# A graph layer's last stage: x1 of half of the rows added on TensorE and kept in PSUM, a quarter of the rows normalised by VectorE

## The chip, the cores and the metric

The kernel runs on one core of a Trainium2 chip. The metric is the device time of one execution in microseconds (us); lower is better. Engines are TensorE (PE; its weight loads are PEld), VectorE (DVE), ScalarE (ACT), GpSimd (POOL) and SyncE (SP), which issues the transfers here. The memory that TensorE writes to is PSUM: 8 banks of 512 fp32 numbers per partition, 128 partitions.

## The reference

`x` is (16, 1024, 256) in fp32: 16 batches, 1024 nodes, 256 channels. Two layers follow each other, each with a residual and a layer norm over the channels:

```python
x = _layernorm(x + _L0_gnn_ref(x, para, adj, kv_w))     # attention over a weighted graph
x = _layernorm(x + _L1_gnn_ref(x, adj, W1, b1, g1, be1, W2, b2, g2, be2))

def _L1_gnn_ref(features, A, W1, b1, g1, be1, W2, b2, g2, be2):
    ...
    agg = jnp.einsum('nm,bmd->bnd', A_hat, features)
    h = jax.nn.relu(_batchnorm(agg.reshape(-1, d) @ W1.T + b1, g1, be1))
    out = h @ W2.T + b2
    out = _batchnorm(out, g2, be2)         # mean and variance over all 16 x 1024 rows
    return out.reshape(b, n, -1)
```

The first layer's output is called x1 below. The change concerns the last line of the first block for layer 1: batch norm of `out`, the sum with x1, and the layer norm. The batch norm needs statistics over all rows, so no row can be finished before the last `out` is known.

## The kernel before

The function `fast_path` does everything (a second function, for denominators out of range, isn't run with these inputs). Layer 0 goes over 16 batches with attention in bursts on TensorE, ScalarE and VectorE, and stores x1 of each batch in DRAM. Then `aht` holds the normalised adjacency, and layer 1 computes the aggregate and the first linear map batch by batch, stores `h` in DRAM and collects statistics in `bn1_st`.

Two stages remain, and they are the ones that the change touches. In both the order of instructions on TensorE, ScalarE and VectorE is the order of the program (`manual_schedule`)[...]. The framework puts in the semaphore waits that the data need.

*Second linear map* (from L1431). For each batch `b`, `h` is loaded (`load_h`, two ahead), ScalarE applies batch norm 1 and relu to it in place (`scale_shift1`, L1387), and TensorE computes `out` transposed, in two halves `c` of 128 channels: eight matmuls of 512 columns (L1456) into a PSUM tile `po` of 1024 columns, which is two banks. VectorE adds the bias `b2` while it copies to `o2T[b]` (L1460) and collects `bn_stats` of both 512-column halves in `bn2_st` (L1464). All 16 `o2T` tiles stay in SBUF, 8 KB per partition each. After the last batch `coefficients2(c)` turns the statistics into a scale `sg2` and a shift `sh2` per channel: `bn_aggr` on VectorE (L1227), five small operations on GpSimd (L587 to L1231).

*Last stage* (from L1473). x1 of a batch comes back from DRAM as `xf[b]`, with 8 groups `n` of 128 rows along the free dimension. Seven buffers hold it: three in pool `xp` (batches 0 to 2, loaded during the stage before) and four in `fin2`. For each batch:

- `scale_shift(b)`: ScalarE applies scale and shift to `o2T[b]` in place, two instructions of 1024 columns (L1485), one for each half of the channels.
- `residual2(b)`: for each of four pairs of row groups, TensorE transposes four 128x128 blocks back to rows (L1497, tile `pf`, one bank; four such tiles take turns), VectorE adds x1 and writes the sum over `xf` (L1502, 512 columns), and takes `bn_stats` of each of the two row groups (L1504). Then GpSimd computes the reciprocal standard deviation and the negative mean times it, for all 8 groups at once, in ten small operations (L1510 to L1519).
- `finish(b)`: ScalarE normalises each of the 8 row groups (L1526, 256 columns), writing over `o2T[b]`, and SyncE stores the batch (L1530) and then loads x1 of batch `b + 7` (L1428) into the buffer that has come free.

The loop at L1536 puts them in the order `residual2(b)`, `scale_shift(b + 1)`, `finish(b - 1)`, so that GpSimd has the time of one batch to make its coefficients.

Of the kernel before, what the change touches and what calls it, by code (L numbers as in the profile page):

```python
# [10 lines left out]
F32 = mybir.dt.float32  # L11
I32 = mybir.dt.int32
AF = mybir.ActivationFunctionType
ALU = mybir.AluOpType
AX = mybir.AxisListType
PSUM = bass.MemoryType.PSUM
DRAM = bass.MemoryType.DRAM

P = 128
HALF = 512  # L20
# [495 lines left out]
def fast_path(  # L516
# [19 lines left out]
    nc = tc.nc  # L536
    B, N, C = x.shape
    H = 4
    D = C // H
    NCH = N // P  # L540
    CC = C // P
    FH = W1.shape[0]
    HC = FH // P
    scale = float((1.0 + 1e-06) / (np.sqrt(D) + 1e-06))

    const = ctx.enter_context(tc.tile_pool(name="const", bufs=1))
# [4 lines left out]
    def open_psum():  # L551

        stack = ExitStack()
        for tag in "sto":
            psum[tag] = stack.enter_context(tc.tile_pool(name=f"ps_{tag}", bufs=2, space=PSUM))
        return stack
# [3 lines left out]
    def tile_s(name):  # L560
        return psum["s"].tile([P, N], F32, tag="s", name=name)

    def tile_t(name):
        return psum["t"].tile([P, HALF], F32, tag="t", name=name)

    def tile_o(name):
        return psum["o"].tile([P, HALF], F32, tag="o", name=name)
# [7 lines left out]
    ident = const.tile([P, P], F32, name="ident")  # L575
# [95 lines left out]
    H0, H1 = slice(0, HALF), slice(HALF, N)  # L671
# [3 lines left out]
    cols = {}  # L675
# [24 lines left out]
    with (  # L700
# [10 lines left out]
        st = {}  # L711
# [404 lines left out]
        with tc.manual_schedule(engines={mybir.EngineType.PE, mybir.EngineType.Activation, mybir.EngineType.DVE}):  # L1116
# [48 lines left out]
            for j in range(len(bursts)):  # L1165
                b, u = j // PERB, j % PERB
# [30 lines left out]
            j = len(bursts)  # L1197
# [14 lines left out]


    w1T, w2T = wl["w1T"], wl["w2T"]
    bn1_st = const.tile([P, HC, 2 * B, 6], F32, name="bn1_st")
    bn2_st = const.tile([P, CC, 2 * B, 6], F32, name="bn2_st")

    def batchnorm(stats, gamma, beta, k, name):

# [15 lines left out]
    with (  # L1235
# [9 lines left out]
        def bank(name):  # L1245
            return ps8.tile([P, HALF], F32, tag="bank", name=name)

        def temps(k):
            return lambda key, name: strt.tile([P, HALF], F32, tag=f"{key}{k}", name=f"{key}_{name}")


        wS = strt.tile([P, 4, C], F32, name="wS")
# [133 lines left out]
        def scale_shift1(h, k):  # L1386
            nc.scalar.activation(  # L1387
                h, h, AF.Relu, bias=sh1[:, k : k + 1], scale=sg1[:, k : k + 1]
            )
# [3 lines left out]
        for k in range(HC):  # L1393
            ps = [bank(f"ph_{k}_{half}") for half in range(2)]
            for c in range(CC):
                for half, hs in enumerate((H0, H1)):
                    nc.tensor.matmul(
                        ps[half], w1T[:, c, k * P : (k + 1) * P], t[:, c, hs],
                        start=(c == 0), stop=(c == CC - 1),
# [11 lines left out]
        nc.gpsimd.dma_start(h_d[B - 1], ht)  # L1411

    graph.close()
    ctx.enter_context(open_psum())

# [2 lines left out]
    with tc.tile_pool(name="o2p", bufs=1) as o2p:  # L1420
        o2T = [
            o2p.tile([P, CC, N], F32, tag=f"o2_{b}", name=f"o2_{b}") for b in range(B)
        ]
        xf = {}

        def load_x1(b, pool, tag):
            xf[b] = pool.tile([P, NCH, C], F32, tag=tag, name=f"xf_{b}")
            nc.sync.dma_start(xf[b], x1_d[b])  # L1428

        coefficients2, sg2, sh2 = batchnorm(bn2_st, cols["g2"], cols["be2"], CC, "bn2")  # L1430
        with (  # L1431
            tc.tile_pool(name="hl", bufs=2) as hl,
            tc.manual_schedule(
                engines={mybir.EngineType.PE, mybir.EngineType.Activation, mybir.EngineType.DVE}
            ),
        ):
            hs_of = {0: h0}

            def load_h(b):
                ht = hl.tile([P, HC, N], F32, tag="hl", name=f"hl_{b}")  # L1440
                nc.sync.dma_start(ht, h_d[b])
                hs_of[b] = [ht[:, k, :] for k in range(HC)]

            load_h(1)
            for b in range(B):
                if b + 2 < B:
                    load_h(b + 2)
                if b + 1 < B:
                    for k in range(HC):
                        scale_shift1(hs_of[b + 1][k], k)  # L1450
                h = hs_of.pop(b)
                for c in range(CC):
                    ps = tile_s(f"po2_{b}_{c}")
                    for k in range(HC):
                        for hs in (H0, H1):
                            nc.tensor.matmul(  # L1456
                                ps[:, hs], w2T[:, k, c * P : (c + 1) * P], h[k][:, hs],
                                start=(k == 0), stop=(k == HC - 1),
                            )
                    nc.vector.tensor_scalar(  # L1460
                        o2T[b][:, c, :], ps, cols["b2"][:, c : c + 1], None, ALU.add
                    )
                    for half, hs in enumerate((H0, H1)):
                        nc.vector.bn_stats(bn2_st[:, c, 2 * b + half, :], o2T[b][:, c, hs])  # L1464
                    if b == B - 1:
                        coefficients2(c)
                if b >= B - 3:
                    load_x1(b - (B - 3), xp, "x")

        with (  # L1473
            tc.tile_pool(name="fin2", bufs=4) as fin2,
            tc.manual_schedule(
                engines={mybir.EngineType.PE, mybir.EngineType.Activation, mybir.EngineType.DVE}
            ),
        ):
            for b in range(3, 7):
                load_x1(b, fin2, "xf")  # L1480

            def scale_shift(b):
                for c in range(CC):
                    o = o2T[b][:, c, :]
                    nc.scalar.activation(  # L1485
                        o, o, AF.Identity, bias=sh2[:, c : c + 1], scale=sg2[:, c : c + 1]
                    )

            def residual2(b):
                xt = xf[b]  # L1490
                st = small.tile([P, NCH, 6], F32, tag="ln_st", name=f"st_l1_{b}")
                for pair in range(NCH // 2):
                    pt = tile_t(f"pf_{b}_{pair}") if pair % 2 else tile_o(f"pf_{b}_{pair}")
                    for j in range(2):
                        n = 2 * pair + j
                        for c in range(CC):
                            nc.tensor.transpose(  # L1497
                                pt[:, j * C + c * P : j * C + (c + 1) * P],
                                o2T[b][:, c, n * P : (n + 1) * P], ident,
                            )  # L1500
                    xs = xt[:, 2 * pair : 2 * pair + 2, :].rearrange("p n c -> p (n c)")
                    nc.vector.tensor_add(xs, pt, xs)  # L1502
                    for n in (2 * pair, 2 * pair + 1):
                        nc.vector.bn_stats(st[:, n, :], xt[:, n, :])  # L1504

                me, qe, mo, qo = (st[:, :, k] for k in (1, 2, 4, 5))
                w = small.tile([P, 4, NCH], F32, tag="ln_w", name=f"w_l1_{b}")
                rstd, nmr, dif, var = (w[:, k, :] for k in range(4))
                pool = nc.gpsimd
                pool.tensor_tensor(nmr, me, mo, ALU.add)  # L1510
                pool.tensor_tensor(dif, me, mo, ALU.subtract)
                pool.tensor_tensor(var, qe, qo, ALU.add)
                pool.tensor_scalar(var, var, 1.0 / C, EPS, ALU.mult, ALU.add)
                pool.tensor_tensor(dif, dif, dif, ALU.mult)
                pool.tensor_scalar(dif, dif, 0.25, None, ALU.mult)
                pool.tensor_tensor(var, var, dif, ALU.add)
                pool.tensor_tensor(rstd, var, mhalf, ALU.pow)
                pool.tensor_tensor(nmr, nmr, rstd, ALU.mult)
                pool.tensor_scalar(nmr, nmr, -0.5, None, ALU.mult)  # L1519
                return rstd, nmr  # L1520

            def finish(b, rstd, nmr):
                xt = xf.pop(b)
                y = o2T[b].rearrange("p c n -> p (c n)").rearrange("p (n c) -> p n c", c=C)
                for n in range(NCH):
                    nc.scalar.activation(  # L1526
                        y[:, n, :], xt[:, n, :], AF.Identity,
                        bias=nmr[:, n : n + 1], scale=rstd[:, n : n + 1],
                    )
                nc.sync.dma_start(out[b].rearrange("(n p) c -> p n c", p=P), y)  # L1530
                if b + 7 < B:
                    load_x1(b + 7, *((fin2, "xf") if 3 <= b < 7 else (xp, "x")))

            scale_shift(0)
            coeffs = {}
            for b in range(B):  # L1536
                coeffs[b] = residual2(b)
                if b + 1 < B:
                    scale_shift(b + 1)
                if b:  # L1540
                    finish(b - 1, *coeffs.pop(b - 1))
            finish(B - 1, *coeffs.pop(B - 1))


# [41 lines left out]
```

## Time and profile before

The time is 2651.31 us, the median of three runs (2650.74 to 2654.38); the profiled execution has a span of 2651.3 us and a mean granted TensorE clock of 0.981.

| engine | busy us | share of the span | instructions |
|---|---|---|---|
| PE | 2553.7 | 96% | 12966 |
| PEld | 1110.1 | 42% | 12966 |
| DVE | 1600.2 | 60% | 2160 |
| ACT | 1126.8 | 43% | 1349 |
| POOL | 336.2 | 13% | 407 |

TensorE is busy nearly throughout, but not at the end: in the page's 40 slices of the span the last two digits of its row are 6 and 4, where the rest are 8 or 9, and the granted clock falls there too. By line, the chain of work that ended last has 8% of the span in L1456, 2% in L1526, and 1% each in L1485 and L1504. A row of the groups reads: line, engine, operation, out<-in by the program's names, shapes, count, then the busy time in us and the mean ns of one, then the idle time just before, with what ended most of it. Shares of the whole span say little on a stage of 120 us; for it the same views are cut to a window.

### The profile page before, as it was taken

Reading aid. Unit: us, or ns where it says so; the run is one execution under the profiler, and the core shown is the slowest. Engines: PE = TensorE matmul, PEld = TensorE weight load, DVE = VectorE, ACT = ScalarE, POOL = GpSimd, SP = SyncE. Lnnn points to the kernel's source line nnn. Section 1 sums busy time; section 2 is a strip of 40 time slices with the busy share of each in tenths; the row PEclk is TensorE's granted clock in tenths of the full one; section 3 lists DMA queues with packets and bytes.
Section 4 is the critical chain, followed back from the end, with each engine's and each line's share of the span. In section 5 each row is a group of like instructions: output and inputs, shape, how many; then the busy total and the mean of one; then the engine's idle time right before and its main releaser. Section 6 shows DMA issues by size and latency. Waiting matters only on the chain. (4 is left out here: it accounts for less than half of the span.)

```text
span 2651.3 us, 31994 instructions
## 1 busy us (share of the span) xinstructions
PE 2553.7 (96%) x12966; PEld 1110.1 (42%) x12966; DVE 1600.2 (60%) x2160; ACT 1126.8 (43%) x1349; POOL 336.2 (13%) x407
## 2 busy tenths in 40 slices
PE   8999999999999999999999999999999999999964
PEld 4443444444434434444444343344444444444443
DVE  5465665756656657666566576765655655533376
ACT  5363563654645636545446354410101001233368
POOL 0001000100100011001000100321222211100044
PEclk9999999999999999999999999999999999999975
DMA  4001101001011011010110110112122122353367
GB/s 143 2 9 41 33 10 41 21 22 33 9 41 33 9 41 33 10 41 3 39 33 9 41 49 1 41 64 95 80 95 95 66 92 82 137 202 143 149 222 240
DMA packets 134557, 168.94 MB, mean 64 GB/s; under 512 B 86785, under 2 KB 120065, under 8 KB 124033
## 3 DMA queue, kind: packets, MB, share of 16 engines
q1 hardware_dynamic: 129568, 116.47, 14.2%
q0 software_dynamic: 4832, 50.34, 4.6%
q8 instruction: 103, 1.69, 0.3%
q14 instruction: 54, 0.43, 0.0%
HBM read 99.36 MB, written 67.44 MB: 63 GB/s over the span
## 5 line engine op out<-in xcount | busy, mean ns | idle before, releaser
L908 ACT ACTIVATE p<-ps 128x1024 f32<-128x1024 f32 x512 | 495.7, 1020 | 179.5 <-PE ps L903 142.9
L933 DVE TENSOR_TENSOR acc<-acc,p 128x1024 f32<-128x1024 f32 x384 | 483.2, 1258 | 61.0 <-ACT p L908 32.4
L903 PE MATMUL ps<-qT,kT 64*64 64x512 f32 x4096 | 490.6, 594 | 1.4 <-ACT p L908 1.4
L924 PE MATMUL po<-p,v 64*64 64x512 f32 x4096 | 485.3, 589 | 0.0
L805 PE MATMUL pg<-wg,x 128*128 128x512 f32 x960 | 425.2, 596 | 0.0
L979 POOL TENSOR_TENSOR x<-x,o 128x512 f32<-128x512 f32 x64 | 109.5, 1711 | 1434.8 <-DVE o L974 1434.8
L924 PEld LDWEIGHTS po<-p,v 64*64 64x64 f32 x4096 | 156.7, 133 | 282.8 <-issue 282.6
L805 PEld LDWEIGHTS pg<-wg,x 128*128 128x128 f32 x960 | 177.6, 190 | 226.9 <-issue 203.3
L903 PEld LDWEIGHTS ps<-qT,kT 64*64 64x64 f32 x4096 | 146.1, 132 | 280.2 <-issue 231.5
L817 ACT ACTIVATE qT<-qT 128x512 f32<-128x512 f32 x64 | 40.3, 631 | 482.0 <-DVE qT L814 481.9
L1456 PE MATMUL po<-hl,w12T 128*128 128x512 f32 x512 | 220.3, 592 | 3.1 <-ACT hl L1387 2.3
L814 DVE SCALAR_TENSOR_TENSOR qT<-pg,para_s 128x512 f32<-128x512 f32 x64 | 43.9, 689 | 271.1 <-PE pg L805 269.8
L793 DVE SCALAR_TENSOR_TENSOR wg<-wg,adj_s 128x1024 f32<-128x1024 f32 x128 | 153.1, 1217 | 15.5 <-ACT wg L789 15.5
L784 ACT ACTIVATE wg<-crow,ccol 128x1024 f32<-128x1024 f32 x128 | 146.6, 1146 | 11.8 <-DMA crow<-c 11.8
L1456 PEld LDWEIGHTS po<-hl,w12T 128*128 128x128 f32 x512 | 97.1, 190 | 126.3 <-issue 120.5
L789 ACT ACTIVATE wg<-wg 128x1024 f32<-128x1024 f32 x128 | 135.5, 1060 | 2.6
L1387 ACT ACTIVATE hl<-hl,bn_sh,bn_sg 128x1024 f32<-128x1024 f32 x64 | 74.3, 1229 | 135.0 <-DMA hl<-h 133.6
L855 PE MATMUL pv<-kvw_s,xT 128*128 128x256 f32 x512 | 124.0, 385 | 1.6 <-ACT kT L846 1.6
L1460 DVE TENSOR_SCALAR o<-po,col_b 128x1024 f32<-128x1024 f32 x32 | 41.1, 1284 | 139.1 <-PE po L1456 139.1
L842 PE MATMUL pk<-xT,kvw_s 128*128 128x512 f32 x256 | 120.3, 592 | 0.0
L855 PEld LDWEIGHTS pv<-kvw_s,xT 128*128 128x128 f32 x512 | 94.9, 190 | 51.9 <-issue 27.6
L1286 PE MATMUL a_agg<-ahT,x1l 128*128 128x512 f32 x240 | 108.1, 593 | 1.1 <-ACT agg L1104 1.1
(151 smaller groups left out, 2625.4 us busy)
## 6 DMA issues: line engine op xcount, KB each, us to landing
h<-hw POOLq DMA_DIRECT2D x16, 2048.0 KB, 6.6
hl<-h SPq DMA_DIRECT2D x15, 2048.0 KB
x<-x POOLq DMA_DIRECT2D x16, 1024.0 KB, 4.2
x1l<-x SPq DMA_DIRECT2D x16, 1024.0 KB
xf<-x SPq DMA_DIRECT2D x16, 1024.0 KB
out_dram<-o SPq DMA_DIRECT2D x16, 1024.0 KB
x<-in_x_dram SPq DMA_DIRECT2D x15, 1024.0 KB
crow<-c SPq DMA_DIRECT2D x15, 512.0 KB
```

What stands on the lines that cost most here:

```text
L784: nc.scalar.activation(w, s["crow"], AF.Abs, bias=s["ccol"][:, n : n + 1])
L789: nc.scalar.activation(w, w, AF.Tanh, scale=0.5)
L793: nc.vector.scalar_tensor_tensor(w, w, 1.0, adj_s[:, n, :], op0=ALU.subtract, op1=ALU.mult)
L805: nc.tensor.matmul(ps, xt[:, n, c * P : (c + 1) * P], s["wg", n][:, hs], start=(n == 0), stop=(n == NCH - 1),)
L842: nc.tensor.matmul(ps, kvw_s[:, c, kc * P : (kc + 1) * P], s["xT"][:, c, hs], start=(c == 0), stop=(c == CC - 1),)
L855: nc.tensor.matmul(pt[:, j * C : (j + 1) * C], s["xT"][:, c, n * P : (n + 1) * P], kvw_s[:, c, C : 2 * C], start=(c == 0), stop=(c == CC - 1),
L903: nc.tensor.matmul(ps[kh * D : (kh + 1) * D, hd * HALF : (hd + 1) * HALF], kT[r, pr, ks], qT[r, pr, qh * HALF : (qh + 1) * HALF], start=Tr ...
L908: nc.scalar.activation(p, ps, AF.Exp)
L924: nc.tensor.matmul(g["po"][kh][hd * D : (hd + 1) * D, :], s["v"][r, m, h * D : (h + 1) * D], p[r, hd * HALF : (hd + 1) * HALF], start=(m = ...
L933: nc.vector.tensor_add(g["acc"], g["acc"], p)
L979: nc.gpsimd.tensor_tensor(xs, xs, o.rearrange("p n h d -> p n (h d)"), ALU.add)
L1456: nc.tensor.matmul(ps[:, hs], w2T[:, k, c * P : (c + 1) * P], h[k][:, hs], start=(k == 0), stop=(k == HC - 1),)
```

## The change

It reorders the end of the kernel in five ways.

- The last bias add (batch 15, second half of the channels) goes from VectorE to ScalarE, in two halves of 512 columns, each in a bank of its own.
- The first `scale_shift(0)` is done in four pieces of 512 columns, first both channel halves of the first four row groups, so that these can be transposed while the rest is scaled.
- For row groups 4 to 7 the sum with x1 is made by TensorE in PSUM: a matmul of `xf` (512 columns, two row groups) with the identity starts the bank (`add_x1`), and the transposing matmuls of `o2T` add to it (`start=False`). They are ordinary matmuls with the identity as moving operand, no longer transposes[...]. The sum stays there, in a tile `held` of two banks, three of which take turns, until `finish`. VectorE's add of these row groups goes; `bn_stats` reads PSUM. For row groups 0 to 3 all is as it was, with two PSUM tiles `ps_sum` in place of four.
- In `finish` VectorE normalises row groups 0 and 1, ScalarE groups 4 to 7 out of PSUM and then 2 and 3.
- The pools of PSUM of the stage before are closed, since `held` and `ps_sum` need all 8 banks; `bn1_st` and `bn2_st` move from the pool of constants to pools that live only as long as they are needed.

The aim is to take work from ScalarE and VectorE, the two busy engines of this stage, and give it to TensorE, which waits there, and to shorten the way from the last matmul to the first residual.

```diff
-    bn1_st = const.tile([P, HC, 2 * B, 6], F32, name="bn1_st")
-    bn2_st = const.tile([P, CC, 2 * B, 6], F32, name="bn2_st")
...
+        bn1_st = strt.tile([P, HC, 2 * B, 6], F32, name="bn1_st")
...
-    ctx.enter_context(open_psum())
+    part_psum = open_psum()
...
+        bn2_st = o2p.tile([P, CC, 2 * B, 6], F32, name="bn2_st")
...
-                    nc.vector.tensor_scalar(
-                        o2T[b][:, c, :], ps, cols["b2"][:, c : c + 1], None, ALU.add
-                    )
+                    if b == B - 1 and c == CC - 1:
+                        for hs in (H0, H1):
+                            nc.scalar.activation(
+                                o2T[b][:, c, hs], ps[:, hs], AF.Identity,
+                                bias=cols["b2"][:, c : c + 1],
+                            )
+                    else:
+                        nc.vector.tensor_scalar(
+                            o2T[b][:, c, :], ps, cols["b2"][:, c : c + 1], None, ALU.add
+                        )
...
+        part_psum.close()
         with (
             tc.tile_pool(name="fin2", bufs=4) as fin2,
+            tc.tile_pool(name="ps_held", bufs=3, space=PSUM) as ps_held,
+            tc.tile_pool(name="ps_sum", bufs=2, space=PSUM) as ps_sum,
...
             def scale_shift(b):
-                for c in range(CC):
-                    o = o2T[b][:, c, :]
+                for hs in (H0, H1) if b == 0 else (slice(0, N),):
+                    for c in range(CC):
+                        o = o2T[b][:, c, hs]
...
+            held = {}
+
+            def add_x1(b, pair):
+                if b not in held:
+                    held[b] = ps_held.tile([P, N], F32, tag="held", name=f"held_{b}")
+                nc.tensor.matmul(
+                    held[b][:, (pair - 2) * HALF : (pair - 1) * HALF], ident,
+                    xf[b][:, 2 * pair : 2 * pair + 2, :].rearrange("p n c -> p (n c)"),
+                    start=True, stop=False, skip_group_check=True,
+                )
+
             def residual2(b):
...
-                for pair in range(NCH // 2):
-                    pt = tile_t(f"pf_{b}_{pair}") if pair % 2 else tile_o(f"pf_{b}_{pair}")
+                for pair in range(2):
+                    pt = ps_sum.tile([P, HALF], F32, tag="sum", name=f"pf_{b}_{pair}")
...
+                for pair in range(2, 4):
+                    if b:
+                        add_x1(b, pair)
+                    pt = held[b][:, (pair - 2) * HALF : (pair - 1) * HALF]
+                    for j in range(2):
+                        n = 2 * pair + j
+                        for c in range(CC):
+                            nc.tensor.matmul(
+                                pt[:, j * C + c * P : j * C + (c + 1) * P],
+                                o2T[b][:, c, n * P : (n + 1) * P], ident,
+                                start=False, stop=True, skip_group_check=True,
+                            )
+                        nc.vector.bn_stats(st[:, n, :], pt[:, j * C : (j + 1) * C])
...
             def finish(b, rstd, nmr):
-                xt = xf.pop(b)
+                xt, hx = xf.pop(b), held.pop(b)
...
-                for n in range(NCH):
+                for n in (0, 1):
+                    nc.vector.tensor_scalar(
+                        y[:, n, :], xt[:, n, :], rstd[:, n : n + 1], nmr[:, n : n + 1],
+                        ALU.mult, ALU.add,
+                    )
+                for n in (4, 5, 6, 7, 2, 3):
                     nc.scalar.activation(
-                        y[:, n, :], xt[:, n, :], AF.Identity,
-                        bias=nmr[:, n : n + 1], scale=rstd[:, n : n + 1],
+                        y[:, n, :], hx[:, (n - 4) * C : (n - 3) * C] if n >= 4 else xt[:, n, :],
+                        AF.Identity, bias=nmr[:, n : n + 1], scale=rstd[:, n : n + 1],
                     )
...
+            add_x1(0, 2)
+            add_x1(0, 3)
             scale_shift(0)
```

More of the change, by code (lines that the diff above doesn't have):

```diff
@@ L1482, in scale_shift @@
             def scale_shift(b):
-                for c in range(CC):
-                    o = o2T[b][:, c, :]
-                    nc.scalar.activation(
-                        o, o, AF.Identity, bias=sh2[:, c : c + 1], scale=sg2[:, c : c + 1]
-                    )
+                for hs in (H0, H1) if b == 0 else (slice(0, N),):
+                    for c in range(CC):
+                        o = o2T[b][:, c, hs]
+                        nc.scalar.activation(
+                            o, o, AF.Identity, bias=sh2[:, c : c + 1], scale=sg2[:, c : c + 1]
+                        )
[8 more added lines that the diff above has]
+                )
             def residual2(b):
@@ L1522, in finish @@
             def finish(b, rstd, nmr):
-                xt = xf.pop(b)
+                xt, hx = xf.pop(b), held.pop(b)
                 y = o2T[b].rearrange("p c n -> p (c n)").rearrange("p (n c) -> p n c", c=C)
-                for n in range(NCH):
+                for n in (0, 1):
+                    nc.vector.tensor_scalar(
+                        y[:, n, :], xt[:, n, :], rstd[:, n : n + 1], nmr[:, n : n + 1],
+                        ALU.mult, ALU.add,
+                    )
+                for n in (4, 5, 6, 7, 2, 3):
                     nc.scalar.activation(
-                        y[:, n, :], xt[:, n, :], AF.Identity,
-                        bias=nmr[:, n : n + 1], scale=rstd[:, n : n + 1],
+                        y[:, n, :], hx[:, (n - 4) * C : (n - 3) * C] if n >= 4 else xt[:, n, :],
+                        AF.Identity, bias=nmr[:, n : n + 1], scale=rstd[:, n : n + 1],
                     )
```

## The prediction

> **What bounds the kernel now.** I read, in this order, the groups of instructions of the last 270 us, the windows of the last stage, the timeline of one batch, and the chain of waits. The change lies behind the last `po` matmul (it ends near 2531.7 us), so only some 120 of the 2651.3 us can move much. First the groups: line, engine, out<-in, count, then busy us and mean ns of one, then idle us and its releaser.
>
> ```profile
> L1526 ACT ACTIVATE o<-xf,w_l 128x256 f32<-128x256 f32 x128 | 64.5, 585 | 8.7 <-POOL w_l L1519 8.7
> L1497 PE MATMUL pf<-ident,o 128*128 128x128 f32 x256 | 57.0, 395 | 43.9 <-ACT o L1485 40.4 <-DVE xf L1502 3.5
> L1504 DVE BATCH_NORM_STATS2 st_l<-xf 128x6 f32<-128x256 f32 x128 | 48.2, 418 | 3.0
> L1502 DVE TENSOR_TENSOR xf<-pf,xf 128x512 f32<-128x512 f32 x64 | 43.3, 677 | 10.4 <-PE pf L1497 6.0 <-issue 4.4
> L1485 ACT ACTIVATE o<-o,bn_sh,bn_sg 128x1024 f32<-128x1024 f32 x32 | 37.6, 1226 | 18.9 <-POOL bn_sh L1231 18.9
> ```
>
> TensorE waits on ScalarE 40.4 us here, ScalarE almost only at the start (18.9 + 8.7). The windows give busy us of PE, PEld, DVE, ACT, POOL, then granted clock, DMA share, GB/s:
>
> ```profile
> 2580.00:2610.00 30.00, 18.12 (x79) 15.31 (x79) 26.36 (x59) 30.00 (x51) 17.18 (x50) 0.61 1.01 338
> 2610.00:2640.00 30.00, 14.28 (x64) 11.84 (x64) 23.56 (x52) 27.73 (x48) 16.99 (x50) 0.61 0.55 186
> ```
>
> ScalarE fills all 30.00 us, VectorE 26.36. The TensorE clock is 0.61 and the DMA share 1.01. One batch in the timeline (start us, us, instruction):
>
> ```profile
> 2604.87 4.03 ACT L1526 ACTIVATE o<-xf,w_l 128x256 f32<-128x256 f32 x8
> 2605.02 3.46 PE L1497 MATMUL pf<-ident,o 128*128 128x128 f32 x15 [0.66 <-ACT o L1485]
> 2606.01 0.69 DVE L1502 TENSOR_TENSOR xf<-pf,xf 128x512 f32<-128x512 f32 x1 [0.51 <-issue]
> 2606.81 0.75 DVE L1504 BATCH_NORM_STATS2 st_l<-xf 128x6 f32<-128x256 f32 x2
> 2607.48 0.67 DVE L1502 TENSOR_TENSOR xf<-pf,xf 128x512 f32<-128x512 f32 x1
> 2608.81 2.36 ACT L1485 ACTIVATE o<-o,bn_sh,bn_sg 128x1024 f32<-128x1024 f32 x2
> 2611.07 4.03 ACT L1526 ACTIVATE o<-xf,w_l 128x256 f32<-128x256 f32 x8
> ```
>
> The period is 2611.07 - 2604.87 = 6.20 us, all ScalarE: eight small activations cost (4.03 - 0.585) / 7 = 0.493 each in a row, 3.94 together, and two large ones 2.26. VectorE's pair period (an add, two statistics) is 1.38 (2607.48 to the next add at 2608.85); four are 5.52. The chain of waits gives the ends (start us, us, what):
>
> ```profile
> 2531.69 1.29 DVE o L1460
> 2533.01 1.30 DVE bn_st L1464 x2
> 2537.15 1.25 ACT o L1485
> 2539.38 0.70 DVE xf L1502
> ...
> 2637.93 1.68 POOL w_l L1517
> 2641.73 2.55 ACT o L1526 x5
> ```
>
> From the last `po` matmul to the first residual add it is 7.7 us. At the end the last statistics finish at 2636.14, GpSimd's ten small operations take 4.1 us, eight activations 4.04 (to 2644.28), the last store 7.0.
>
> [...] here the 128x512 copy from PSUM (L1017) takes 685 ns and the add of two SBUF operands (L666) 682, so I add nothing.
>
> **The change, part by part.**
>
> *Start.* ScalarE does the last bias add in halves (687 ns each by L1404, the same form), the first one matmul (0.43 us) before the last ends, and statistics of the first half overlap the second: statistics end near 2533.3 instead of 2534.3, 1.05 us earlier. The first scale and shift needs 0.63 (L817, 128x512) instead of 1.25 before TensorE may start. First residual add at 2539.4 - 1.05 - 0.6, about 2537.6. The two x1 matmuls of batch 0 lie in TensorE's wait for the coefficients: free.
>
> *ScalarE per batch:* 6 x 0.493 + 2.26 = 5.22, instead of 6.20. *VectorE's own work:* two pairs 2.76, four statistics at 0.335 (0.75 for two, less the tail) 1.34, two normalisations at 0.323 (L600, same form, eight in 2.67 us) 0.65: 4.75. By busy time all gets shorter.
>
> *The new wait.* For rows 4 to 7 the loop now writes row n with two transposing matmuls, and reads row n for its statistics, before it writes row n+1. Rows 4 and 5 share a bank, and 6 and 7. [...] the matmuls of row 5 must wait for the statistics of row 4, those of row 7 for row 6. Behind them in TensorE's queue stand the x1 matmul of the other bank, rows 6 and 7, and the whole next batch; VectorE waits for each in turn. Costs of the links:
> - statistics to matmul: 0.42 for the instruction + 0.05 (2546.96 to 2547.01 for add to transpose);
> - two matmuls to the statistics. Three transposes took 0.59 to VectorE's start at full clock (2561.62 to 2562.21) and 1.00 at half (2605.01 to 2606.01); one fewer is 0.11 or 0.21 less: 0.48 and 0.79. These are no longer in transpose mode; their weight load is 190 ns (L855) instead of 140 (L970) at full clock, so I add 0.07: 0.55 full, 0.86 half;
> - an x1 matmul of 512 columns: 0.43 full (220.3 us / 512), 0.85 half.
>
> From the start t of row 4's statistics, full clock / half clock: row 5's at t + 0.47 + 0.55 = 1.02 / 1.33. TensorE meanwhile streams row 5, the x1 matmul and row 6: 0.47 + 0.33 + 0.43 + 0.3 + 0.22 = 1.75 / 0.47 + 0.57 + 0.85 + 0.48 + 0.27 = 2.64, when row 6's statistics start. Row 7's follow 1.02 / 1.33 later: 2.77 / 3.97. Then 0.335 and the two normalisations 0.65: 3.76 / 4.96. With the 2.76 of the two pairs the period is 6.52 / 7.72. The next batch's first transposes fit behind row 7's statistics (ready near 3.4 / 4.8). Before had 6.20, so VectorE and TensorE in alternation become the bound and ScalarE's 0.98 us is worth nothing. I take the mean of the clocks, 7.1: this stage had full clock in about a fifth of its time at 0.61[...].
>
> *Sum.* Batch 0 needs no x1 matmul in the chain and no normalisation: about 5.8. Batch 1 starts at 2543.4, batch 15 at 2543.4 + 14 x 7.1 = 2642.8; its last statistics end 2.76 + 3.4 + 0.42 later, 2649.4. Then GpSimd 4.1, six activations 5 x 0.493 + 0.585 = 3.05, the store 7.0: 2663.6, rounded 2664. At full clock all through 2655, at half 2673. The last finish is 1.0 shorter than before; the normalisation by VectorE runs beside it.
>
> *Nothing gained or lost:* PSUM pools reopened (banks long read; the wait for coefficients hides it), three held tiles (one is freed two batches before it is asked for), the statistics tiles moved between pools (addresses only). DMA: nine load and store pairs at the 338 GB/s of before are 6.2 us each; a period of 7.1 asks for less.
>
> **Rivals.**
> - *No wait inside a bank* (only true overlaps of columns are ordered): then ScalarE sets 5.22, batch 15 starts at 2537.6 + 4.7 + 14 x 5.22 = 2615.4, its statistics end 4.3 later, plus 14.15: 2634. DMA, which is full at 338 GB/s, would end no earlier: 9 x 6.2 + 7 stores of about 3.4 from 2551.5 is 2631, and the last store's latency: so 2636. For it: the work by engine[...].
> - *Wait, but full clock:* 2655, about no change. [...] against it: 0.61 now with similar idle shares.
> - *Wait at half clock throughout:* 2673. [...]
>
> **How the numbers follow.** Wait with mixed clock (2658 to 2670) 0.66, with full clock (2650 to 2658) 0.09, with half clock (2670 to 2676) 0.10, no wait (2634 to 2641) 0.15. The range 2652 to 2676 holds 0.66 + 0.10 + most of 0.09, over 0.8. Above 2656.6 (0.2% over 2651.3) lie 0.66 + 0.10 + 0.03 = 0.79; within 0.2% 0.06; faster 0.15.
>
> **What would show it.** Right: in the changed profile the matmuls of rows 5 and 7 wait on the statistics, VectorE idles on them by some 2 to 3 us a batch, ScalarE has gaps, and the activations recur every 6.5 to 7.7 us. Start step: first add near 2537.6. Wrong: ScalarE without gaps and a period near 5.2; or a clock near 1.0; or VectorE waiting for the first transposes of a batch rather than for rows 5 to 7.

## The result, and the profile after

The changed kernel takes 2700.7 us, the median of four runs (2699.72 to 2703.64), against 2652.85 (2650.74 to 2655.2) for the kernel before beside it: a ratio of 1.0182, 95% interval 1.0164 to 1.02. It is slower, as the prediction said, but by 48 us where 12.7 were predicted; the time lies outside the range of 2652 to 2676. The profiled execution has a span of 2698.7 us.

The groups of the changed kernel's last 320 us (line, engine, operation, out<-in, shapes, count, then busy us and mean ns of one, then idle us just before and its releasers):

```profile
L1537 PE MATMUL held<-ident,o 128*128 128x128 f32 x256 | 52.4, 338 | 34.7 <-DVE st_l L1542 34.5 <-ACT o L1499 0.2
L1508 PE MATMUL held<-xf,ident 128*128 128x512 f32 x64 | 45.9, 810 | 9.2 <-DVE st_l L1542 7.9 <-ACT o L1463 1.4
L1569 ACT ACTIVATE o<-held,w_l 128x256 f32<-128x256 f32 x64 | 30.9, 563 | 74.8 <-POOL w_l L1557 69.4 <-DVE st_l L1542 5.4
L1542 DVE BATCH_NORM_STATS2 st_l<-held 128x6 f32<-128x256 f32 x64 | 27.4, 428 | 68.6 <-PE held L1537 68.6
L1522 PE MATMUL pf<-ident,o 128*128 128x128 f32 x128 | 21.2, 320 | 2.3 <-ACT o L1499 2.3
```

Three things are to be seen. VectorE now waits 68.6 us for the matmuls of `held` (L1542 on L1537), 4.3 a batch where 2 to 3 were forecast, and TensorE 34.5 + 7.9 us for the statistics (L1537 and L1508 on L1542): each waits for the other. ScalarE, which waited 8.7 us in its normalisation before, waits 74.8. And the counts: the code calls L1537 128 times (8 in each of 16 batches), the trace has 256; it calls L1508 32 times, the trace has 64. The transposes, L1522, are 128 in both.

A window of the last stage (busy us of PE, PEld, DVE, ACT, POOL, then granted clock, DMA share, GB/s):

```profile
2580.00:2610.00 30.00, 20.61 (x91) 14.34 (x90) 15.94 (x40) 17.07 (x26) 11.30 (x32) 0.81 0.63 211
```

ScalarE went from 30.00 of 30 us to 17.07, VectorE from 26.36 to 15.94, and no engine is full any more. The last part of one batch, in the timeline (start us, us, instruction, idle before and its releaser), shows the alternation:

```profile
2556.03 0.42 DVE L1542 BATCH_NORM_STATS2 st_l<-held 128x6 f32<-128x256 f32 x1
2556.50 0.71 PE L1537 MATMUL held<-ident,o 128*128 128x128 f32 x4 [2.08 <-DVE st_l L1542]
2557.25 0.43 DVE L1542 BATCH_NORM_STATS2 st_l<-held 128x6 f32<-128x256 f32 x1 [0.80 <-PE held L1537]
2557.74 2.08 PE L1508 MATMUL held<-xf,ident 128*128 128x512 f32 x2 [0.52 <-DVE st_l L1542]
2559.60 1.06 PE L1537 MATMUL held<-ident,o 128*128 128x128 f32 x4
2560.70 0.43 DVE L1542 BATCH_NORM_STATS2 st_l<-held 128x6 f32<-128x256 f32 x1 [3.02 <-PE held L1537]
2561.19 0.71 PE L1537 MATMUL held<-ident,o 128*128 128x128 f32 x4 [0.53 <-DVE st_l L1542]
2561.94 0.43 DVE L1542 BATCH_NORM_STATS2 st_l<-held 128x6 f32<-128x256 f32 x1 [0.81 <-PE held L1537]
2562.92 0.69 DVE L1527 TENSOR_TENSOR xf<-pf,xf 128x512 f32<-128x512 f32 x1
```

The four statistics are those of rows 4 to 7. Row 5's matmuls start 0.05 us after row 4's statistics end, row 7's after row 6's: the wait that was predicted. But the x1 matmul of the *other* bank (L1508, for rows 6 and 7) also starts only at 2557.74, 0.06 after row 5's statistics end. It was predicted to run beside them.

The chain of waits of the changed kernel at the start of the stage (start us, us, what):

```profile
2529.31 0.70 ACT o L1463
2530.03 1.30 DVE bn_st L1472 x2
2534.17 0.82 ACT o L1499
2535.62 0.70 DVE xf L1527
```

The last `po` matmul ends at 2529.27, so the way from it to the first residual add is 6.35 us, against 7.71 before (2531.67 to 2539.38). The tail, from the end of the last statistics (2684.33) to 2698.7, is 14.37.

**Where the time went.** The adds of the first pair of each batch recur every 9.35 us on average from batch 1 to batch 15 ((2675.34 - 2544.47) / 14); before it was 6.11 ((2630.45 - 2544.91) / 14, with 6.20 once steady).

### The profile page after: what moved, and what is told of

Read it like the earlier page. It is cut to its first block, busy times and chain, and to the rows that moved or that the text cites. A ratio compares the mean times of both kernels' runs of the same rounds, so it can differ in the third digit from the quotient of the medians.

```text
span 2698.7 us, 32309 instructions
## 1 busy us (share of the span) xinstructions
PE 2601.3 (96%) x13158; PEld 1138.4 (42%) x13158; DVE 1591.6 (59%) x2159; ACT 1111.1 (41%) x1321; POOL 339.0 (13%) x407
## 3 DMA queue, kind: packets, MB, share of 16 engines
q8 instruction: 105, 1.72, 0.3%
## 5 line engine op out<-in xcount | busy, mean ns | idle before, releaser
L817 ACT ACTIVATE qT<-qT 128x512 f32<-128x512 f32 x64 | 40.0, 630 | 482.0 <-DVE qT L814 482.0
L1457 PE MATMUL po<-hl,w12T 128*128 128x512 f32 x512 | 220.3, 593 | 3.3 <-ACT hl L1387 2.6
L855 PEld LDWEIGHTS pv<-kvw_s,xT 128*128 128x128 f32 x512 | 95.1, 190 | 52.9 <-issue 27.6
```

The costliest lines, as they stand in the source:

```text
L855: nc.tensor.matmul(pt[:, j * C : (j + 1) * C], s["xT"][:, c, n * P : (n + 1) * P], kvw_s[:, c, C : 2 * C], start=(c == 0), stop=(c == CC - 1),
L1457: nc.tensor.matmul(ps[:, hs], w2T[:, k, c * P : (c + 1) * P], h[k][:, hs], start=(k == 0), stop=(k == HC - 1),)
```

## The experiments

Two theories stood at the outset. A: the alternation of TensorE and VectorE in `held` costs the time, since reads and writes of the whole two-bank tile are kept in order, and since the links are longer than I took them (an ordinary fp32 matmul is two instructions in the trace). B: it is the amount of work that TensorE was given, in whatever order. The table has all runs (e3 and e8 leave out a part of the work): the median, the ratio to the kernel before on the same chip with its 95% interval, and the mean time from batch to batch (batch 1 to 15, first add to first add).

| run | us | ratio | us per batch |
|---|---|---|---|
| the change | 2700.7 | 1.0182 (1.0164 to 1.02) | 9.35 |
| e1_two_tiles | 2681.83 | 1.0107 (1.009 to 1.0124) | 7.98 |
| e2_stats_last | 2636.36 | 0.9936 (0.9919 to 0.9953) | 5.17 |
| e3_wait_single_pass | 2667.05 | 1.0049 (1.0032 to 1.0066) | 7.02 |
| e4_start_only | 2654.1 | 1.0001 (0.9992 to 1.0009) | 6.14 |
| e5_pair_stats_one_tile | 2666.77 | 1.0044 (1.0027 to 1.0061) | 7.15 |
| e6_pair_stats_two_tiles | 2632.29 | 0.9918 (0.9902 to 0.9935) | 5.06 |
| e7_vector_rows_only | 2653.06 | 0.9994 (0.9986 to 1.0003) | 6.16 |
| e8_wait_two_pass | 2692.95 | 1.014 (1.0123 to 1.0157) | 8.61 |
| e9_two_tiles_all_on_scalar | 2649.0 | 0.998 (0.9973 to 0.9987) | 5.95 |

### e1: `held` as two tiles of one bank

```diff
-            tc.tile_pool(name="ps_held", bufs=3, space=PSUM) as ps_held,
+            tc.tile_pool(name="ps_held", bufs=6, space=PSUM) as ps_held,
...
-                    held[b] = ps_held.tile([P, N], F32, tag="held", name=f"held_{b}")
+                t = ps_held.tile([P, HALF], F32, tag="held", name=f"held_{b}_{pair}")
+                held.setdefault(b, []).append(t)
...
```

> The changed kernel with the held PSUM tile split into two tiles of one bank each (six take turns), all orders as they are. In the trace of the changed kernel the x1 matmul of the second bank starts 0.05 us after the statistics of row 5 end, though these read the other bank. Theory A (the framework orders writes after reads over a whole tile): that matmul no longer waits, some 0.48 us a batch go (0.43 for the statistics and 0.05), 7 us in all: 2692 to 2695 us, and the x1 matmul starts before the statistics of row 5. Theory B (only the bank counts, and the wait has another cause): no change, 2699 to 2702 us.

It takes 2681.83 us. One batch in its timeline:

```profile
2579.74 0.71 PE L1537 MATMUL held<-ident,o 128*128 128x128 f32 x4 [0.53 <-DVE st_l L1542]
2580.29 1.02 PE L1508 MATMUL held<-xf,ident 128*128 128x512 f32 x2
2580.49 0.43 DVE L1542 BATCH_NORM_STATS2 st_l<-held 128x6 f32<-128x256 f32 x1 [0.81 <-PE held L1537]
2581.80 0.43 DVE L1542 BATCH_NORM_STATS2 st_l<-held 128x6 f32<-128x256 f32 x1 [0.87 <-PE held L1537]
```

The x1 matmul of the second bank (2580.29) now starts before row 5's statistics (2580.49), right behind row 5's matmuls, so its wait was one for the tile and not for the bank. From row 5's statistics to row 6's it is 1.31 us here and 2.09 in a batch of the change at full clock (2576.68 to 2578.77, granted clock 1.00): the wait for the tile is worth 0.78 a batch there. The mean fell by 1.37, more than expected. The rest of it goes with the clock: batches at full clock fell from 8.30 to 7.51 (2552.53 to 2567.55 has two, whose outer links take 1.22 to 1.24, as in the change at a granted clock of 0.99), by 0.79, while the mean stands 0.47 above the full-clock batch here and 1.05 in the change; from 2560 to 2590 the granted clock is 0.89 here and 0.81 there.

### e2: the statistics of rows 4 to 7 after all their matmuls

```diff
-                        nc.vector.bn_stats(st[:, n, :], pt[:, j * C : (j + 1) * C])
+                for n in range(4, 8):
+                    nc.vector.bn_stats(st[:, n, :], held[b][:, (n - 4) * C : (n - 3) * C])
```

> The changed kernel with the statistics of rows 4 to 7 issued after all matmuls of these rows. Same instructions, same arithmetic. Theory A (the alternation of writes and reads in a tile is the loss): TensorE runs a batch without stopping, 8 transposes, 4 x1 instructions and 16 transposing ones, at full clock about 0.9 + 1.7 + 2.0 = 4.7 us, so ScalarE's 5.2 or so sets the period: 2635 to 2650 us, faster than the kernel before. Theory B (the doubled fp32 instructions on TensorE are the loss whatever the order): at half clock they need 9.1 us, the period stays near 9, 2680 us or more.

It takes 2636.36 us, faster than before by 0.64%, with exactly the instructions of the change. Its window:

```profile
2560.00:2590.00 30.00, 27.11 (x168) 20.11 (x166) 27.71 (x70) 29.84 (x48) 21.20 (x58) 1.00 1.05 401
```

ScalarE is full again (29.84), TensorE is busy for 27.11 of 30 us at a clock of 1.00. Theory B falls: the same TensorE work, in another order, goes through in 5.17 us a batch. (Its clock is higher too, but at full clock a batch of the change still takes 8.30.)

### e3 and e8: the wait alone, with one or two instructions to a link

Both leave out x1 for rows 4 to 7, so TensorE has no x1 matmul; the rest of the change is kept. e3 fills `held` with transposes, e8 with ordinary matmuls. The diff of e3 (in e8 the call stays `nc.tensor.matmul`, with `start=True`):

```diff
-                    if b:
-                        add_x1(b, pair)
...
-                            nc.tensor.matmul(
+                            nc.tensor.transpose(
                                 pt[:, j * C + c * P : j * C + (c + 1) * P],
                                 o2T[b][:, c, n * P : (n + 1) * P], ident,
-                                start=False, stop=True, skip_group_check=True,
                             )
...
-            add_x1(0, 2)
-            add_x1(0, 3)
```

> The changed kernel with rows 4 to 7 written by plain transposes, without x1: it leaves out the sum with x1 for half of the rows, and each block is one TensorE instruction and not two. The alternation with the statistics stays. Theory A (my prediction's chain was right for one pass and only the second pass and the x1 matmuls were missed): three links of 0.42 + 0.05 + 0.48 (full clock) or 0.79 (half), period 6.6 to 7.5 us, 2652 to 2668 us, slower than before though TensorE does no more than before. Theory B (the wait is harmless without the added TensorE work): ScalarE's 5.2 us, about 2635 us.

> The changed kernel, its alternation kept, without the x1 matmuls: rows 4 to 7 are written by ordinary matmuls with the identity (two TensorE instructions a block), and the sum with x1 is left out for half of the rows. Against the run with single-pass transposes it has the second pass alone. The links of the changed kernel were 1.22 (full clock) and 1.75 us (half) from statistics to statistics; three of them, with 2.76 and 0.98: 7.4 to 9.0 us a batch against 6.9 there, 2672 to 2695 us. The rest up to the changed kernel's 9.35 us is then the x1 matmuls in the chain. If the second pass were hidden, it would stay at 6.9 us and 2667 us.

e3 takes 2667.05 us, e8 2692.95. In e3's timeline, at full clock (1.00 is granted in 2602 to 2605, where the links take 0.94 and 0.97):

```profile
2576.60 0.43 DVE L1541 BATCH_NORM_STATS2 st_l<-held 128x6 f32<-128x256 f32 x1 [0.54 <-PE held L1537]
2577.09 0.44 PE L1537 MATMUL held<-ident,o 128*128 128x128 f32 x2 [0.53 <-DVE st_l L1541]
2577.57 0.43 DVE L1541 BATCH_NORM_STATS2 st_l<-held 128x6 f32<-128x256 f32 x1 [0.53 <-PE held L1537]
```

and in e8's, at half clock (0.50 is granted in 2596 to 2602, where they take 1.73 to 1.75):

```profile
2580.68 0.43 DVE L1542 BATCH_NORM_STATS2 st_l<-held 128x6 f32<-128x256 f32 x1 [1.31 <-PE held L1537]
2581.17 1.22 PE L1537 MATMUL held<-ident,o 128*128 128x128 f32 x4 [0.53 <-DVE st_l L1542]
2582.42 0.43 DVE L1542 BATCH_NORM_STATS2 st_l<-held 128x6 f32<-128x256 f32 x1 [1.31 <-PE held L1537]
```

Two calls are x2 in e3 and x4 in e8; the expectations call each of these instructions a pass. The link from statistics to statistics is 0.97 in e3 and 1.74 in e8. The prediction had 0.95 at full clock for transposes (0.47 + 0.48), 1.02 and 1.33 at full and half clock for ordinary matmuls. So my link was right for one instruction to a call, which these matmuls are not. By the means: the wait with single instructions is 7.02 us a batch, already above the 6.11 of before; the second instruction of each link adds 1.59; the x1 matmuls, with their own wait, another 0.74 to 9.35. The clock differs between these runs: it is 0.64 and 0.76 in two windows of e3 (2560 to 2590, 2590 to 2620) and 0.60 and 0.62 in the same ones of e8. But the second instruction costs as much where all three links of a batch are at their longest: with links of 1.19 to 1.22 a batch takes 7.37 to 7.38 in e3 (three from 2550.77), with links of 1.73 to 1.75 it takes 8.97 to 8.98 in e8 (two from 2567.21), 1.60 apart.

### e5 and e6: statistics after each pair, with one tile or two

Both take the statistics of a pair once its eight instructions are through; e6 has besides the two tiles of e1. The diff of e5:

```diff
-                        nc.vector.bn_stats(st[:, n, :], pt[:, j * C : (j + 1) * C])
+                    for j in range(2):
+                        nc.vector.bn_stats(st[:, 2 * pair + j, :], pt[:, j * C : (j + 1) * C])
```

> The changed kernel with the statistics of rows 4 and 5 after the matmuls of both, likewise 6 and 7; the held tile is still one tile of two banks. Within a bank nothing is written after a read any more. Theory A (writes wait for reads of the whole tile): the matmuls of the second bank still wait for the statistics of row 5, once a batch: from row 4's statistics t, 0.34 + 0.42 + 0.05, then 2 x1 instructions and 8 transposing ones (0.86 + 1.05 + 0.2 at full clock, 1.7 + 2.0 + 0.3 at half), two statistics and two normalisations 1.3: period 2.76 + 4.2 to 6.1 = 7.0 to 8.9 us, 2662 to 2690 us. Theory B (only the bank counts): no wait is left, ScalarE's 5.1 us as with all statistics last, 2634 to 2640 us.

> The same order of statistics, the held tile split into two tiles of one bank. Theory A and theory B alike: no matmul waits for statistics of its own batch, ScalarE's 5.1 us, 2633 to 2640 us. The pair of these two runs differs by the tile's size alone: theory A wants 25 us or more between them, theory B none.

e5 takes 2666.77 us, e6 2632.29: 34 us apart, with the same instructions in the same order on every engine, and only the size of the PSUM tile different. In e5's timeline the second bank's x1 matmul waits for the first bank's statistics:

```profile
2578.22 0.75 DVE L1543 BATCH_NORM_STATS2 st_l<-held 128x6 f32<-128x256 f32 x2
2579.02 1.13 PE L1508 MATMUL held<-xf,ident 128*128 128x512 f32 x2 [1.04 <-DVE st_l L1543]
2581.08 0.76 DVE L1543 BATCH_NORM_STATS2 st_l<-held 128x6 f32<-128x256 f32 x2 [2.11 <-PE held L1537]
```

That is 1.04 us of TensorE and then 2.11 of VectorE, once a batch. It shows that the order is kept over the whole tile. The clock is not what parts the two runs: where e5 has a granted clock of 1.00 (2590 to 2620) its batches take 6.93 us, against 5.06 in e6, which has 1.00 as well; that is 1.87 of the 2.09 between the means. In e6's window nothing of the kind is left, and ScalarE fills it:

```profile
2560.00:2590.00 30.00, 27.56 (x168) 20.40 (x168) 28.22 (x72) 30.00 (x48) 21.66 (x60) 1.00 1.05 400
```

e6 is the fastest version here: 0.82% below the kernel before, and some 68 us below the change as it was made.

### e4 and e7: the parts that need no x1 matmul

e4 is the kernel before with the two edits of the start (the last bias add in halves on ScalarE, the first scale and shift in four pieces). e7 adds to it that VectorE normalises two rows of each batch:

```diff
-                for n in range(NCH):
+                for n in range(2):
+                    nc.vector.tensor_scalar(
+                        y[:, n, :], xt[:, n, :], rstd[:, n : n + 1], nmr[:, n : n + 1],
+                        ALU.mult, ALU.add,
+                    )
+                for n in range(2, NCH):
```

> The kernel before with only the two edits of the start: the last bias add in halves on ScalarE and the first scale and shift in four pieces. Prediction's step: 1.05 + 0.6 us less from the last po matmul to the first residual add, 2649 to 2650.5 us against some 2651.5. In the trace of the changed kernel the way was 6.4 us (2529.27 to 2535.62) against 7.7. If ScalarE waited for the whole PSUM tile the first 0.43 us would be missing: 1.3 us less.

> The kernel before with the two edits of the start and with VectorE normalising row groups 0 and 1; x1 is added by VectorE for all rows as before. ScalarE has 6 x 0.493 + 2.26 = 5.2 us a batch, VectorE 5.52 + 0.65 = 6.17 and its first wait of up to 0.5. If busy time decides: period 6.2 to 6.6 us, 2650 to 2657 us, no gain without taking the add away from VectorE. A rival, that ScalarE's relief alone is the gain, wants 5.2 to 5.5 us and 2637 to 2642 us.

e4 takes 2654.1 us beside 2654.05: in the total the start can't be told from nothing (interval 0.9992 to 1.0009). The chain of waits shows more:

```profile
2531.93 0.69 ACT o L1462
...
2536.79 0.82 ACT o L1493
...
2538.60 0.70 DVE xf L1510
```

The last `po` matmul ends at 2531.90, and the first half of the bias add starts at 2531.93, though its own bank was written two instructions earlier. An order over the whole tile would do that; no run splits `po` to test it. The way to the first add is 6.70 us instead of 7.71. The change itself has 6.35, and the 0.35 between them lies in the first transposes: 0.94 us here (2537.66 to 2538.60) and 0.93 in before at a granted clock of 0.50 (2538.45 to 2539.38), 0.59 at 1.00 there (2535.03 to 2535.62), where the x1 matmuls of batch 0 run in the wait for the coefficients. A part of what e4 won is lost again after the start: ScalarE's last normalisation starts at 2639.81 in e4 and at 2640.24 in before, and 0.4 us is below what the total can tell.

e7 takes 2653.06 us (0.9986 to 1.0003), no clear gain. Its window:

```profile
2560.00:2590.00 30.00, 17.88 (x78) 14.43 (x76) 29.31 (x69) 25.82 (x40) 18.11 (x50) 0.61 1.02 341
```

VectorE is at 29.31 of 30: with x1's add still on it, two rows more make it the bound, at 6.16 us a batch.

### e9: e6, with all rows normalised by ScalarE

```diff
-                for n in (0, 1):
-                    nc.vector.tensor_scalar(
...
-                for n in (4, 5, 6, 7, 2, 3):
+                for n in (4, 5, 6, 7, 0, 1, 2, 3):
```

> The version with two tiles and statistics after each pair (2632 us, a batch each 5.07 us), but ScalarE normalises all eight row groups and VectorE none. It undoes one of the two halves of the change's aim. ScalarE has 4 more of these a batch from PSUM and 4 from SBUF, 4 x 0.455 + 4 x 0.493 + 2.3 = 6.1 us; VectorE only 4.1. If ScalarE's sum sets the period: 5.07 + 0.98 = 6.05 us, 15 x 0.98 + 1.0 at the end = 16 us more, 2647 to 2650 us, near the kernel before. If TensorE set the 5.07 us: no change, 2632 us.

It takes 2649.0 us, 0.998 of before (0.9973 to 0.9987). Its window:

```profile
2560.00:2590.00 30.00, 24.07 (x140) 17.39 (x140) 21.02 (x50) 30.00 (x51) 17.06 (x50) 1.00 1.03 347
```

ScalarE is full at 6.04 us a batch once steady (2560 on), and VectorE has 9 us to spare. So the two halves of the change need each other: VectorE's rows without the x1 matmuls give nothing that stands clear of the noise (e7), the x1 matmuls without VectorE's rows about 5 us (e9), both about 23 (e6).

## Why the prediction was right in sign and wrong in size

**What bounds the kernel before: right.** e6 and e9 have ScalarE full as before had, and between them the batch is shorter by 0.98 us (6.04 to 5.06), which is what two rows cost on ScalarE by the prediction (2 x 0.493).

**The new wait: there as forecast, the costs of its links wrong.** The failing step is in "The new wait", in two of its terms.

- *"two matmuls to the statistics ... 0.55 full, 0.86 half" and "an x1 matmul of 512 columns: 0.43 full (220.3 us / 512), 0.85 half".* I divided by a row's count and took that for the number of matmuls. The groups of before have this row, which the prediction used without looking at its count:

```profile
L1456 PE MATMUL po<-hl,w12T 128*128 128x512 f32 x512 | 220.3, 592 | 3.1 <-ACT hl L1387 2.3
```

The code calls L1456 256 times (8 for each of 2 halves and 16 batches). In the trace an ordinary fp32 matmul is two instructions on TensorE (512 for these 256 calls), a transpose is one (L1522, 128 for 128). The x1 matmul is thus an estimated 0.86 at full clock and 1.72 at half (twice 220.3 us / 512, and twice that), and the two matmuls of a row take 0.75 to the statistics at full clock (2556.50 to 2557.25) and 1.25 at half (e8, 2581.17 to 2582.42). What each of the two does the trace doesn't show.

- *"TensorE meanwhile streams row 5, the x1 matmul and row 6".* It doesn't. That the wait goes by bank was an assumption of mine: the last stage of before doesn't show it, since there the reader of a bank comes after all its writers. The runs show the order kept over the whole tile of two banks (e1, where 2.09 becomes 1.31; e5 against e6, 34 us apart), so the x1 matmul of the second bank stands behind row 5's statistics. Whether the other waits, of row 5 on row 4 and of row 7 on row 6, are due to the bank or to the tile stays open: no run has a tile smaller than a bank.

A batch of the change whose links ran at full clock (adds at 2572.69 and 2580.99; granted clock 0.99 from 2574.50 on) shows both, step by step, against the 6.52 of the prediction:

| step | predicted | measured | where |
|---|---|---|---|
| two pairs, to row 4's statistics | 2.76 | 2.77 | 2572.69 to 2575.46 |
| row 4's to row 5's | 1.02 | 1.22 | to 2576.68 |
| row 5's to row 6's | 0.73 | 2.09 | to 2578.77 |
| row 6's to row 7's | 1.02 | 1.24 | to 2580.01 |
| row 7's, two normalisations, next add | 0.99 | 0.98 | to 2580.99 |
| sum | 6.52 | 8.30 | |

Of the 1.78 that is missing, 1.36 is one link. Its split by e1, where the same link takes 1.31 at full clock: 0.78 the wait for the tile, the other 0.58 what is left above the predicted 0.73, which I put down to the second instructions of the x1 matmul and of row 6.

**The mean over the clocks: too low.** I put 0.6 on the full-clock period (7.1); measured it is 1.05 (9.35 against 8.30). It falls mostly on the same link: over batches 1 to 14, row 5's statistics to row 6's takes 2.89 on average instead of 2.09, which is 0.80 of the 1.05. In the batch shown above, 9.66 us long, it is 3.45, which is the whole difference, and there the x1 matmul's two instructions take 1.86 instead of 0.96. The granted clock in 2557.50 to 2559.60 is 0.52, after 1.00 in the 4.5 us ahead of it. That it rises with the work of TensorE was an assumption behind my mean. The runs fit it at the upper end: from 2560 to 2590 the clock is 1.00 in e2, e6 and e9, with TensorE busy for 24 to 27.6 of 30 us. Below that busy time alone does not order them: from 2590 to 2620 it is 0.83 in the change with TensorE busy for 21.7 us, 0.76 in e3 with 16.2 and 0.62 in e8 with 20.9. No run sets the clock by itself, so what lowers it, the waits or something else, was not shown. Nor is the clock the whole loss: at full clock a batch takes 8.30, still above the 6.11 of before.

**The sum.** The profiled span is 35.1 us above the 2663.6 of the prediction: first add 2.0 earlier; batch 0 8.85 instead of 5.8, +3.05 (its three links take 1.74 each at a granted clock of 0.50); 14 batches of 2.25 more, +31.5; batch 15 up to the end of its statistics 8.99 instead of 6.58, +2.4; the tail 14.37 instead of 14.15, +0.2. That is 35.15, the 35.1 but for rounding.

**The start: gain right, its parts not.** The way is shorter by 1.36, against 1.65 predicted; that the first add is even 2.0 ahead of the prediction is because the stage before, up to its last matmul, ended 2.4 us earlier in this profile (2529.27 instead of 2531.67), which I don't put down to the change: over the eleven profiles this point lies between 2529.27 and 2534.22. "The first one matmul before the last ends" didn't come about: both halves start after the last matmul (2529.31), as they would by an order over the whole `po` tile. The statistics end 2.06 after it (2531.33) instead of 2.63 before, 0.57 won instead of 1.05. A piece of scale and shift takes 0.82 instead of the 0.63 taken from L817; even so the first add comes 1.45 after the first piece starts (2534.17 to 2535.62) instead of 2.23, 0.78 won instead of 0.6: 0.43 by the shorter piece, and 0.35 because the first transposes ran at full clock (1.00, where before has 0.50), which no term of mine had. So it is in part luck that the gain comes near.

**The other terms.** VectorE's own work held (2.77 and 0.98 for 2.76 and 0.99), and the tail to 0.2 us. PSUM as a source cost VectorE nothing in the statistics, as assumed: 418 ns in e6 and 419 in e2, the same form from SBUF 418 and 419. ScalarE without waits needs 5.06 us a batch in e6, where I had 5.22.

**The rivals.** "No wait inside a bank" was given 2636 us at a chance of 0.15. It didn't happen, but e2 and e6, which have no wait between the links, take 2636.36 and 2632.29, so its sum was sound. Its DMA limit was not: 338 GB/s is what before moved with ScalarE full, and e2 and e6 moved 401 and 400. "Wait at half clock", at 2673, and "Wait, but full clock", at 2655, fell by the same links as the forecast: the full-clock batch is 8.30 where 6.52 was taken.

## What to carry to other kernels

Hold the count of each row against the calls in the code before dividing by it: an operation can be more instructions than it has calls (L1456: 512 for 256). Where one engine writes a tile in pieces and another reads each piece, what stands behind in both queues can be held up by the tile, as here (1.04 and then 2.11 us a batch in e5), so give each piece a tile of its own and let the reader come after several writes; here that alone turned 48 us lost into 23 won. Work taken off the busiest engine pays only up to the next one (in e7 VectorE, busy for 29.31 of 30 us), so look at how far both are relieved: e7 and e9 each brought little, and together they brought most.

## What the runs showed of the hardware that I had not expected

- An ordinary fp32 matmul, one call in the code, appears in the trace as two TensorE instructions (x512 for 256 calls, x256 for 128, x64 for 32), each 0.43 us at 512 columns (220.3 us / 512) and a granted clock of 1.00 (before, 2300 to 2530); a transpose as one (x128 for 128).
- The transfers were not at a ceiling at 338 GB/s with a share of 1.01: e2 and e6 moved 401 and 400 GB/s at 1.05.
- The granted clock stood at 1.00 over whole windows of 30 us in e2, e6 and e9, while before, with TensorE busy for 18 us of 30, had 0.60. A transpose's mean is 280 ns in e6 (L1522) and 395 in before (L1497).
